# Layer 2: the next image's keys' term in eight steps that begin one chunk earlier, and the choice's subtraction moved from GpSimd to VectorE in seven steps

## The chip, the core and the metric

The kernel runs on one core of a Trainium2 chip. Its engines are TensorE (PE: matmuls; PEld: its weight loads), VectorE (DVE), ScalarE (ACT: activation functions), GpSimd (POOL) and SyncE (SP, which here issues the DMAs). The metric is the device time of one execution in microseconds (us).

## The reference, cut to what matters

A stack of four layers runs on four images of 56 x 56 tokens with 128 channels. The change touches layer 2, and a step that layer 2 and layer 3 share:

```python
def _L2_attn_ref(x, W1, b1, w2, b2):      # x: layer-normalized tokens of an image
    f = jnp.einsum('bih,ha->bia', x, W1[:h])          # the queries' term
    g = jnp.einsum('bjh,ha->bja', x, W1[h:])          # the keys' term
    t = jnp.tanh(f[:, :, None, :] + g[:, None, :, :] + b1)
    scores = jnp.einsum('bija,a->bij', t, w2[:, 0]) + b2[0]
    flag = jnp.tril(jnp.ones((n_seq, n_seq), dtype=x.dtype), -1)[None, :, :]
    e = jnp.exp(scores) * flag
    w = e / (jnp.sum(e, axis=-1, keepdims=True) + 1e-10)
    return jnp.einsum('bij,bjh->bih', w, x)

def _L2_ffn_ref(x, gate_w, gate_b, weight1, weight2):
    probs = jax.nn.softmax(logits, axis=1)            # over an image's tokens, 64 experts
    vals, idx = jax.lax.top_k(probs.transpose(0, 2, 1), K)   # each expert's 8 tokens
    pooled = jnp.einsum('bked,bke->bed', gathered, topv)
    ...
```

Every pair of a query and an earlier key takes 16 tangents, so an image of 3136 tokens costs some 79 million of them.

## The kernel before, in words

**The attention.** An image is 28 tiles of 112 tokens. Queries go in four chunks of seven tiles (784 columns), k = 0 to 3, and for each chunk the key tiles J run from 0 to the chunk's last tile: 7, 14, 21 and 28 of them. Keys lie by eights on the partitions (8 keys x 16 hidden values), so a key tile is 14 groups; four quarters q of a key tile have 4, 4, 3 and 3 of them. A quarter is a *piece*; there are 280 pieces to an image and 1120 in all. For J past the chunk's first tile the causal mask cuts off queries, and the pieces get narrower by 112 columns with each J, from 784 down to 112.

A piece goes through four engines. `adds` (line 1004, DVE) writes up to four sums of the queries' term `fT` and one column of the keys' term `g` into a buffer `th`, of which there are three. `tangents` (L1013, ACT) takes the tanh in place. `scores` (L1024, PE) multiplies by w2 and gathers the rows into a PSUM tile. Once per J, `weights` (L1035 and L1038, ACT) takes the exponential, POOL multiplies the diagonal tile by the mask (L1042), and `weighted` (L1051, PE) sums the values, in quarter 1 of the next J.

**The order.** The program order of these engines is written out by hand in one loop over the pieces. For piece i it issues `tangents(i)`, then at most one extra step, then `adds` of piece i + 2, then `scores(i)`, then (in quarters 0 and 1) `weights` or `weighted` of the J before. The extra step is taken from three lists:

```python
if now and not held:
    now.pop(0)()
elif later_on and q % 2 and not held:
    later_on.pop(0)()
elif behind:
    step = behind.pop(0)
    step()
    held = step.holds
```

`now` holds the end of the chunk before (two copies and four additions to the image, from quarter 2 of J 0 on) and the queries' term of the next chunk of the same image (at J 2). `later_on` is served in odd quarters only. `behind` holds the choice of the image before, filled at J 2 of chunk 0 of images 1 to 3, and in image 3 the experts' matmuls after it.

**`prepare_image`** makes what the next image needs: 14 steps of statistics, a root (`rstd`: ACT loads another table for the square root, and back), 14 steps of normalization into `xa`, seven turns into `xT` (four PE transposes into the PSUM bank "m" and a copy that goes to DVE and ACT by turns, L141 and L143), a memset on POOL and `keys`: eight matmuls of 128 x 392, which read every eighth column of `xT`, into "m", and the addition of b1 on DVE (L972). An fp32 matmul shows as two passes in the trace. The 38 steps come at J 2 of the last chunk, k = 3, with the queries' term of the next image behind them. `xT` has one buffer. The first image is prepared ahead of the loop.

PSUM is full: one bank "m", one bank "h", four for the scores, two for the weighted sums. "h" serves the choice and the experts through `hold`, the fourth of `pools`.

**`choose_steps`** makes an image's choice of tokens in two halves of slots, one slot for each extra step. The first half normalizes, turns and multiplies by the gate. The second, on tiles of 64 experts x 3136 tokens, takes the largest value (slot 1), the exponential, the shares and the eight largest (`eight`, slot 7), replaces those by zero in a copy `M` (`replaced`, slot 8, L1266), and subtracts the copy from the shares, so that `M` keeps the chosen values alone (`left`, slot 9, L1271 on POOL); `M` then goes to DRAM over SP's queue (L1272). Slots 10 and up normalize the tokens again (`norm`, L1219; `c_xa` has three buffers), turn `M` (L1278, copied by ACT, L1284) and pool the tokens (`pool`, L1291); a `norm` waits for the `pool` that frees its buffer. The tiles of the width of an image, `wide`, have two buffers, which the experts' weights (L1330, 1 MB each, over SP) use afterwards. The choice of image 3 is made in layer 3, where a slot that does not hold takes two units of that layer's loop.

Of the kernel before, what the change touches and what calls it, by code (L numbers as in the profile page):

```python
# [17 lines left out]
B, HW, C = 4, 56, 128  # L18
S = HW * HW
P = 128  # L20
# [3 lines left out]
CH = TC * TP  # L24
NCH = S // CH
# [18 lines left out]
JG = P // AH  # L44
# [62 lines left out]
class Hybrid:  # L107
# [764 lines left out]
    def layer2_attention(self):  # L872
# [3 lines left out]
        nc, a, tc = self.nc, self.a, self.tc  # L876
        ET = mybir.EngineType
        with ExitStack() as ctx:
# [5 lines left out]
            wg = self.t(wp, [P, JG, P], "wg")  # L884
# [3 lines left out]
            for j in range(JG):  # L888
                own = slice(j * AH, (j + 1) * AH)
# [12 lines left out]
            ps_h = ctx.enter_context(tc.tile_pool(name="l2_h", bufs=1, space=PSUM))  # L902
# [3 lines left out]
                tc.manual_schedule(engines={ET.PE, ET.Activation, ET.DVE, ET.Pool})  # L906
            )
            m = lambda: self.t(ps_m, [P, 512], "m")
            pools = self.f2_wide, self.f2_sm, m, lambda: self.t(ps_h, [P, 512], "h")
            self.w2 = self.experts2_weights(self.f2_w, m)  # L910
            root = lambda var: self.rstd(sm, var, [TP, NT], 1e-5, "ln")
            im, fT, po, ps, th, es = {}, {}, {}, {}, {}, {}

            chunks = [(t, min(WT, NT - t)) for t in range(0, NT, WT)]
            order = [(b, k) for b in range(B) for k in range(len(chunks))]
# [12 lines left out]
            def halves(lo, hi):  # L928
                return [(i // HALF, max(lo - i, 0), HALF) for i in range(0, hi, HALF) if lo < i + HALF]

            def prepare_image(b):

                r = im[b] = {}
                x = self.X[b]

                def stats(t0):
                    if t0 == 0:
                        r["xa"] = self.t(big, [TP, NT, C], "xa")
                        r["mv"] = self.t(sm, [TP, NT, 2], "ln_mv", bufs=1)
                    for t in range(t0, t0 + 2):  # L940
                        st = self.t(sm, [TP, nc.vector.BN_STATS_DIM], "ln_st", bufs=4)
                        nc.vector.bn_stats(st, x[:, t, :])
                        nc.vector.bn_aggr(r["mv"][:, t, :], st)

                def root():
                    r["r"] = self.rstd(sm, r["mv"][:, :, 1], [TP, NT], 1e-5, "ln")

                def norm(t0):
                    for t in range(t0, t0 + 2):
                        nc.vector.tensor_scalar(  # L950
                            r["xa"][:, t, 0:C], x[:, t, :], r["mv"][:, t, 0:1], r["r"][:, t : t + 1],
                            op0=ALU.subtract, op1=ALU.mult,
                        )

                def turn(c):
                    if c == 0:
                        r["xT"] = self.t(big, [P, S], "xT", bufs=1)
                    self.transposed_chunk(ps_m, "m", r["xa"], c, r["xT"][:, c * CH : (c + 1) * CH])

                def ones():  # L960
                    nc.gpsimd.memset(r["xa"][:, :, C - 1 : C], 1.0)

                def keys():
                    ps = m()
                    for j in range(JG):
                        nc.tensor.matmul(
                            ps[:, : S // JG], wg[:, j, :],
                            r["xT"].rearrange("p (g j) -> p g j", j=JG)[:, :, j],
                            start=(j == 0), stop=(j == JG - 1),
                        )  # L970
                    r["g"] = self.t(big, [P, S // JG], "g")
                    nc.vector.tensor_scalar(r["g"], ps[:, : S // JG], b1, None, op0=ALU.add)  # L972

                bind = lambda f, *args: lambda: f(*args)
                return (
                    [bind(stats, t) for t in range(0, NT, 2)] + [root]
                    + [bind(norm, t) for t in range(0, NT, 2)] + [bind(turn, c) for c in range(NCH)]
                    + [ones, keys]
                )

            def queries(j):

                b, k = order[j]
                t, n = chunks[k]
                fT[j] = self.t(sm, [P, WT * TP], "fT")
                for i, _, w in halves(0, n * TP):
                    ps = m()[:, :w]
                    at = t * TP + i * HALF
                    nc.tensor.matmul(
                        ps, wf.rearrange("p j a -> p (j a)"), im[b]["xT"][:, at : at + w],  # L990
                        start=True, stop=True,
                    )
                    nc.vector.tensor_copy(fT[j][:, i * HALF : i * HALF + w], ps)
# [15 lines left out]
            def tangents(i):  # L1009
                j, J, q = pieces[i]  # L1010
                lo, hi = span(j, J)
                own = th[i][:, 0 : len(groups(q)), lo:hi]
                nc.scalar.activation(own, own, AF.Tanh)  # L1013

            def scores(i):
                j, J, q = pieces[i]
                if q == 0:
                    ps[j, J] = self.t(ps_s, [P, 2, 512], "s")
                off = QW - JG - JG * q
                z = th.pop(i)  # L1020
                for h, lo, hi in halves(*span(j, J)):
                    for blk, n in groups(q):
                        rows = min(QW, TP - QW * blk)
                        nc.tensor.matmul(  # L1024
                            ps[j, J][QW * blk : QW * blk + rows, h, lo:hi], place[:, off : off + rows],
                            z[:, blk, h * HALF + lo : h * HALF + hi],
                            start=(q == 0), stop=(n + 1 == NG or q == TC - 1),
                        )
# [48 lines left out]
            now, later_on, behind, held = [], [], [], False  # L1077
# [4 lines left out]
            def add_ahead(i):  # L1082
                if i < len(pieces):
                    j = pieces[i][0]
                    if i == first[j] and j not in fT:
                        while later_on:
                            later_on.pop(0)()
                        queries(j)
                    adds(i)
# [3 lines left out]
            for i, (j, J, q) in enumerate(pieces):  # L1093
                tangents(i)
                b, k = order[j]
                if J == 2 and q == 0 and j + 1 < len(order):
                    if order[j + 1][1]:
                        now.append(lambda j=j: queries(j + 1))
                    else:
                        later_on += prepare_image(order[j + 1][0])  # L1100
                        later_on.append(lambda j=j: queries(j + 1))
                if k == 0 and J == 2 and q == 0 and b:


                    behind += self.choose_steps(
                        b - 1, self.f2_pooled[:, :, b - 1], self.w2, pools, root
                    )
                    if b == B - 1:
                        behind += self.experts2_steps(
                            range(B - 1), self.f2_pooled, self.w2, pools, 3, lambda: None  # L1110
# [10 lines that stand above are left out]
                add_ahead(i + 2)  # L1121
                scores(i)
                before = pieces[i - TC][:2] if i >= TC else None
                if before and q == 0:
                    weights(*before)
                if before and q == 1:
                    weighted(*before)
                    if before[0] != j:
                        now += attended(before[0])
            j, J, _ = pieces[-1]  # L1130
# [64 lines left out]
    def choose_steps(self, b, pooled, w, pools, root):  # L1195


        nc = self.nc
        wide, sm, m, hold = pools
        x = self.X[b]  # L1200
        r = {}
        bind = lambda f, *args: lambda: f(*args)
# [64 lines left out]
                out=r["M"], in_to_replace=r["top"], in_values=r["pr"], imm_value=0.0  # L1267
            )

        def left():  # L1270
            nc.gpsimd.tensor_sub(r["M"], r["pr"], r["M"])  # L1271
            nc.sync.dma_start(out=w["M"][b], in_=r["M"])  # L1272

        def turn_places(c):
            r["pm", c] = m().rearrange("p (k e) -> p k e", k=TC)
# [20 lines left out]
        def pooled_out():  # L1296
            nc.vector.tensor_copy(pooled, r["pp"][:, :E2])

        over = lambda f: [bind(f, c) for c in range(NCH)]
# [3 lines left out]
            (15, 2, over(logits)), (16, 2, over(biased)),  # L1303
        )
        second = self.in_line(
            (1, 2, [largest, exp, shares, eight]), (8, 1, [replaced]), (9, 1, [left]),
            (10, 2, over(norm)), (13, 2, over(turn_places), True), (14, 2, over(turned_places)),
            (16, 2, over(pool)), (30, 1, [pooled_out]),
        )
        return first + second  # L1310

# [471 lines left out]
```

## Time and profile before

| | us |
|---|---|
| runs shown (3): median, lowest, highest | 8102.83, 8095.14, 8106.98 |
| profiled execution: its time, its span | 8105.82, 8104.0 |
| busy in the span: PE, PEld | 6852.8, 2722.9 |
| busy in the span: DVE, ACT, POOL | 5831.0, 5182.0, 2999.5 |
| layer 2: first to last tangent | 3730 to 6559 |
| tangents L1013, 1120 of 2.09 us | 2294.5 |
| adds L1004, 3920 of 0.56 us | 1935.0 |
| scores L1024, 14336 matmuls | 1490.7 |

The profile is one execution of the program. In the groups of instructions a row gives line, engine, operation, the tile written and the tiles read with their shapes, the count, then the busy time and the mean length of one in ns, then the engine's idle time just before them and what ended most of it. In a timeline a row gives the start, the length, engine, line and operation, the count of those merged, and in brackets the idle time before it and who ended it. A row of windows gives start and end of a stretch, its length, the busy time and number of instructions of PE, PEld, DVE, ACT and POOL, then TensorE's granted clock, the share of DMA engines busy and GB/s.

### The profile page before, as it was taken

The page shows a single profiled execution, that of the slowest core. Times are in us where ns is not written, and L with a number is a line of the kernel's source. Part 1 is how long each engine was busy: PE and PEld are TensorE (multiplying, and loading weights), DVE is VectorE, ACT ScalarE, POOL GpSimd, SP SyncE. Part 2 cuts the span into 40 slices and gives each one's busy share as a digit, 9 for nine tenths or more (in the row PEclk, how much of TensorE's full clock was granted, in tenths as well). Part 3 has the DMA queues.
Part 4 walks back from the last instruction along what each step waited for, and adds up shares of the span by engine and source line. Part 5 has one row for each costly group of instructions (what it writes and reads, how often), then busy time and mean ns, then how long its engine had stood idle before and what let it go on. Part 6 is the DMA issues. An engine that isn't in the chain of part 4 may idle for free.

```text
span 8104.0 us, 106345 instructions
## 1 busy us (share of the span) xinstructions
PE 6852.8 (85%) x41037; PEld 2722.9 (34%) x41037; DVE 5831.0 (72%) x10065; ACT 5182.0 (64%) x5084; POOL 2999.5 (37%) x2081
## 2 busy tenths in 40 slices
PE   8878998999899989996777777777777879999999
PEld 4442333333333333332222222222222334444544
DVE  6777887888788788886787878777787754434444
ACT  4545555556565556555998899889889964333332
POOL 4547887888788788880000000000011000000000
PEclk9989998999899889998999899999989989999999
DMA  2000000000000000000000000000003101210000
GB/s 53 1 13 1 1 1 1 1 1 1 1 1 1 1 1 1 1 1 5 1 1 1 5 1 1 1 5 1 1 26 116 45 6 39 86 63 5 5 6 6
DMA packets 85494, 102.39 MB, mean 13 GB/s; under 512 B 21158, under 2 KB 50742, under 8 KB 84279
## 3 DMA queue, kind: packets, MB, share of 16 engines
q1 hardware_dynamic: 84985, 95.58, 4.0%
q8 instruction: 322, 5.28, 0.3%
q14 instruction: 187, 1.53, 0.1%
HBM read 85.28 MB, written 10.29 MB: 12 GB/s over the span
## 4 chain that ended last, share of the span: by engine, by line
PE 38%; ACT 17%; POOL 15%; issue 14%; DVE 10%; DMA 0%; SPq 0%; ACTq 0%; DVEq 0%; POOLq 0%
ACT th L1013 12%; POOL hs L690 10%; PE q L1555 7%; PE o L1566 6%; PE s L1024 6%; DVE th L1004 5%; POOL dBu L673 4%; PE a L654 3%; PE o L1051 3%; PE pe L1720 2%; PE m L792 2%; PE y L696 1%; PE u L663 1%; PE m L728 1%; DVE hs L685 1%
## 5 line engine op out<-in xcount | busy, mean ns | idle before, releaser
L1013 ACT ACTIVATE th<-th 128x3136 f32<-128x3136 f32 (+12 forms) x1120 | 2294.5, 2094 | 220.1 <-DVE th L1004 166.1
L1004 DVE TENSOR_SCALAR th<-fT,g 128x784 f32<-128x784 f32 (+6 forms) x3920 | 1935.0, 561 | 475.1 <-PE s L1024 442.1
L1024 PE MATMUL s<-th,place 128*32 128x392 f32 (+7 forms) x14336 | 1490.7, 492 | 712.1 <-ACT th L1013 708.9
L685 DVE TENSOR_TENSOR_SCAN hs<-a,dBu 128x896 f32<-128x896 f32 x896 | 1795.8, 2014 | 282.2 <-ACT a L668 272.4
L690 POOL TENSOR_TENSOR hs<-hs,bc 128x896 f32<-128x896 f32 x896 | 1842.2, 2083 | 68.8 <-DVE hs L685 40.3
L668 ACT ACTIVATE a<-a 128x896 f32<-128x896 f32 x896 | 811.4, 906 | 805.4 <-PE u L663 607.4
L663 PE MATMUL u<-du,pick 32*128 32x448 f32 x3584 | 988.2, 626 | 99.2 <-ACT dBu L672 51.8
L654 PE MATMUL a<-delta,A_pick 32*128 32x448 f32 x3584 | 1007.5, 612 | 6.8 <-DVE hs L685 6.1
L1024 PEld LDWEIGHTS s<-th,place 128*32 128x32 f32 (+1 forms) x14336 | 423.8, 111 | 1647.3 <-ACT th L1013 1126.4
L1560 ACT ACTIVATE e<-q,shift 128x448 f32<-128x448 f32 (+1 forms) x700 | 441.5, 634 | 739.8 <-PE q L1555 739.4
L678 DVE TENSOR_TENSOR dBu<-u,bc 128x896 f32<-128x896 f32 x616 | 663.5, 1077 | 168.3 <-PE u L663 167.4
L673 POOL TENSOR_TENSOR dBu<-dBu,bc 128x896 f32<-128x896 f32 x280 | 583.7, 2084 | 434.0 <-ACT dBu L672 434.0
L1566 PE MATMUL o<-e,xk 128*128 128x448 f32 (+1 forms) x1400 | 655.7, 550 | 29.3 <-ACT oT L1541 29.3
L1042 POOL TENSOR_TENSOR e<-e,later 112x112 f32<-112x112 f32 x112 | 79.2, 707 | 1602.3 <-ACT e L1035 968.6
L1555 PE MATMUL q<-xT 128*128 128x448 f32 (+1 forms) x1400 | 658.4, 553 | 7.8 <-ACT e L1560 7.8
L1725 DVE SCALAR_TENSOR_TENSOR X<-pe,r_gate,X 112x128 f32<-112x128 f32 x896 | 313.9, 351 | 462.1 <-PE pe L1720 426.1
L654 PEld LDWEIGHTS a<-delta,A_pick 32*128 32x128 f32 x3584 | 316.4, 193 | 545.4 <-issue 253.8
L696 PE MATMUL y<-hs,sum 128*32 128x448 f32 x3584 | 453.1, 577 | 3.0 <-POOL hs L690 3.0
L1051 PE MATMUL o<-e,xa 112*128 112x392 f32 (+5 forms) x1024 | 425.7, 538 | 1.1 <-POOL e L1042 1.1
L663 PEld LDWEIGHTS u<-du,pick 32*128 32x128 f32 x3584 | 285.8, 193 | 327.4 <-DVE dBu L678 195.0
L1566 PEld LDWEIGHTS o<-e,xk 128*128 128x128 f32 (+1 forms) x1400 | 264.1, 192 | 315.8 <-issue 277.2
L1654 POOL MEMSET lc_xa<- 112x4 f32 x28 | 3.1, 110 | 933.7 <-DVE lc_xa L1648 666.4
(253 smaller groups left out, 7688.0 us busy)
## 6 DMA issues: line engine op xcount, KB each, us to landing
wide<-in_L_ffn_weight SPq DMA_DIRECT2D x64, 1024.0 KB
X<-in_x SPq DMA_DIRECT2D x8, 784.0 KB
out<-X SPq DMA_DIRECT2D x28, 224.0 KB
M<-wide SPq DMA_DIRECT2D x4, 784.0 KB
wide<-M SPq DMA_DIRECT2D x4, 784.0 KB
e_edge<-dtab SPq DMA_DIRECT2D x42, 49.0 KB
cw<-in_L_conv_conv_w SPq DMA_DIRECT2D x1, 1024.0 KB
c_h<-in_L_ffn_weight SPq DMA_DIRECT2D x16, 64.0 KB
```

The source lines that it names most:

```text
L654: nc.tensor.matmul(halves(A[p])[:, k], w["A"][own, order[j][2], f, q, :], pre[j]["delta"][own, f], start=True, stop=True,)
L663: nc.tensor.matmul(halves(U[p + 1])[:, k], w["pick"][own, q, :], pre[j]["du"][own, f], start=True, stop=True,)
L668: nc.scalar.activation(A[p], A[p], AF.Exp)
L673: nc.gpsimd.tensor_mul(v, v, pre[j]["bc"][:, 0:1].to_broadcast([P, 2, CH]))
L685: nc.vector.tensor_tensor_scan(flat, A.pop(p), V.pop(p), 0.0, op0=ALU.mult, op1=ALU.add)
L690: nc.gpsimd.tensor_mul(HS[p], HS[p], bc[:, 1:2].to_broadcast([P, 2, CH]))
L1004: nc.vector.tensor_scalar(th[i][:, blk, lo:hi], fT[j][:, lo:hi], im[order[j][0]]["g"][:, at : at + 1], None, op0=ALU.add,)
L1013: nc.scalar.activation(own, own, AF.Tanh)
L1024: nc.tensor.matmul(ps[j, J][QW * blk : QW * blk + rows, h, lo:hi], place[:, off : off + rows], z[:, blk, h * HALF + lo : h * HALF + hi], s ...
L1051: nc.tensor.matmul(po[j][:, h, lo:hi], im[b]["xa"][:, J, :], e[:, h * HALF + lo : h * HALF + hi], start=(J == 0), stop=(J == t + ((h + 1) ...
L1555: nc.tensor.matmul(ps[:n, :CH], xT[b][:, k : k + n], xT[b][:, c * CH : (c + 1) * CH], start=True, stop=True,)
L1566: nc.tensor.matmul(po[b, c], xk[b][:n, t, :], es.pop((b, c, t))[:n], start=(t == 0), stop=(t == N - 1))
```

## The change

`prepare_image` is put on `later_on` from J 6 of the last chunk but one (k = 2) on, where the choice is done. Its last step becomes nine: eight steps of one matmul each, which accumulate in bank "h" in place of "m", and one for the addition of b1. The queries' term of the next image is still put on the list at J 2 of the last chunk.

In the choice, `left` is split into seven steps of 448 tokens on DVE; the store follows the seventh. `replaced` moves from slot 8 to 10, the seven steps of `left` take slots 11, 13 and so on to 23, and all later stages move by two slots, from a last slot of 30 to one of 32.

```diff
-            pools = self.f2_wide, self.f2_sm, m, lambda: self.t(ps_h, [P, 512], "h")
+            hold = lambda: self.t(ps_h, [P, 512], "h")
+            pools = self.f2_wide, self.f2_sm, m, hold
...
-                def keys():
-                    ps = m()
-                    for j in range(JG):
-                        nc.tensor.matmul(
-                            ps[:, : S // JG], wg[:, j, :],
-                            r["xT"].rearrange("p (g j) -> p g j", j=JG)[:, :, j],
-                            start=(j == 0), stop=(j == JG - 1),
-                        )
+                def keys(j):
+                    if j == 0:
+                        r["ps"] = hold()
+                    nc.tensor.matmul(
+                        r["ps"][:, : S // JG], wg[:, j, :],
+                        r["xT"].rearrange("p (g j) -> p g j", j=JG)[:, :, j],
+                        start=(j == 0), stop=(j == JG - 1),
+                    )
+
+                def keyed():
+                    ps = r["ps"]
                     r["g"] = self.t(big, [P, S // JG], "g")
                     nc.vector.tensor_scalar(r["g"], ps[:, : S // JG], b1, None, op0=ALU.add)
...
-                    + [ones, keys]
+                    + [ones] + [bind(keys, j) for j in range(JG)] + [keyed]
...
                     else:
-                        later_on += prepare_image(order[j + 1][0])
                         later_on.append(lambda j=j: queries(j + 1))
+                if J == 6 and q == 0 and k == len(chunks) - 2 and b + 1 < B:
+                    assert not behind
+                    later_on += prepare_image(b + 1)
...
-        def left():
-            nc.gpsimd.tensor_sub(r["M"], r["pr"], r["M"])
-            nc.sync.dma_start(out=w["M"][b], in_=r["M"])
+        def left(c):
+            own = slice(c * CH, (c + 1) * CH)
+            nc.vector.tensor_sub(r["M"][:, own], r["pr"][:, own], r["M"][:, own])
+            if c == NCH - 1:
+                nc.sync.dma_start(out=w["M"][b], in_=r["M"])
...
-            (1, 2, [largest, exp, shares, eight]), (8, 1, [replaced]), (9, 1, [left]),
-            (10, 2, over(norm)), (13, 2, over(turn_places), True), (14, 2, over(turned_places)),
-            (16, 2, over(pool)), (30, 1, [pooled_out]),
+            (1, 2, [largest, exp, shares, eight]), (10, 1, [replaced]), (11, 2, over(left)),
+            (12, 2, over(norm)), (15, 2, over(turn_places), True), (16, 2, over(turned_places)),
+            (18, 2, over(pool)), (32, 1, [pooled_out]),
```

## The prediction

> **What bounds the kernel now.** The page comes first: which engine is busiest overall does not decide, because the change lies in layer 2 alone, slices 19 to 33 of 40, where the page's slices give ACT eights and nines and PE and DVE sevens and eights. The groups of instructions say what fills ACT there: the tangents.
>
> ```profile
> L1013 ACT ACTIVATE th<-th 128x3136 f32<-128x3136 f32 (+12 forms) x1120 | 2294.5, 2094 | 220.1 <-DVE th L1004 166.1
> ```
>
> There are 1120 pieces, four to a key tile J. I took the start of the first tangent of every J from the timeline: a full-width J (784 query columns) without extra work takes 10.40 us, all of it ACT. Stretches that are longer are what can be won. Windows over three neighbouring J at the passage from image 2 to image 3 (the last chunk, J 20, 21, 22) give busy time by engine:
>
> ```profile
> 5762.20:5772.60 10.40, 7.13 (x56) 2.65 (x52) 8.14 (x15) 9.41 (x6) 0.25 (x1) 1.00 0.01 2
> 5772.60:5794.80 22.20, 20.12 (x92) 5.98 (x92) 6.79 (x13) 11.35 (x7) 0.00 (x0) 1.00 0.00 0
> 5794.80:5803.80 9.00, 7.53 (x51) 2.46 (x48) 7.58 (x16) 8.35 (x4) 0.00 (x0) 1.00 0.01 3
> ```
>
> J 21 takes 22.2 instead of 10.4, with PE full and ACT half idle. The timeline names the cause:
>
> ```profile
> 5780.60 11.51 PE L966 MATMUL m<-xT,wg 128*128 128x392 f32 x16
> 5792.15 0.63 DVE L972 TENSOR_SCALAR g<-m,b 128x392 f32<-128x392 f32 x1 [12.05 <-PE m L966]
> 5793.62 0.91 ACT L1035 ACTIVATE e<-s,b 112x784 f32<-112x784 f32 x1 [10.58 <-PE s L1024]
> ```
>
> The keys' term is 16 matmul passes in one step; the scores queue behind them, and DVE's sum waits for them at the head of its own queue. All three passages (4347, 5063, 5781 us) show J 21 at 22.2.
>
> The choice is read in the same way: the sixth J of chunk 1 in image 1 (first row) against the same J in image 0, which has no choice to make (second row).
>
> ```profile
> 4547.40:4569.60 22.20, 8.50 (x72) 2.56 (x66) 20.95 (x18) 10.68 (x5) 7.06 (x1) 0.86 0.12 25
> 3847.70:3858.10 10.40, 7.32 (x64) 2.36 (x60) 7.80 (x14) 10.40 (x6) 0.00 (x0) 1.00 0.01 2
> ```
>
> Here DVE is full. The timeline again:
>
> ```profile
> 4555.81 3.40 DVE L1266 MATCH_REPLACE8 wide<-c_top,wide 64x3136 f32<-64x3136 f32 x1
> 4559.14 10.38 DVE L1004 TENSOR_SCALAR th<-fT,g 128x784 f32<-128x784 f32 x7
> 4559.35 7.06 POOL L1271 TENSOR_TENSOR wide<-wide 64x3136 f32<-64x3136 f32 x1 [81.24 <-DVE wide L1266]
> 4567.49 4.97 ACT L1013 ACTIVATE th<-th 128x2352 f32<-128x2352 f32 x2 [9.41 <-DVE th L1004]
> ```
>
> Seven adds take 10.38 us where they take 3.85 elsewhere; one of them has the length of POOL's subtraction (the longest add of the kernel is 7.17 us). ACT is idle 9.41. It recurs at 5276 and 5993.
>
> **What the Trainium skill says.** SBUF — State Buffer, "Reading the diagram": DVE and GpSimd share a port pair under an exclusive lock, and the loser waits for the whole instruction. The trace agrees: an add of 0.6 us lasts 7.17 beside the 7.06 us subtraction. Perfetto Trace Analysis, "Optimizing Scalar/DVE Operations": breaking up an instruction that causes bubbles elsewhere may let work finish sooner. The 10.58 us bubble is of that kind, though on PE. VectorE: DVE Perf Modes, the section on the TRN2 errata, prices an fp32 sum of two tensors at (N+151)/0.96 ns: an estimate of 624 ns for 448 columns. The trace has no such row on DVE; its rows of 28 columns (0.186 us) and 896 (1.068) interpolate to 0.61. Neighbours overlap (the 784-wide add reads 0.63 and comes every 0.56), so I take 0.56 on the queue.
>
> **The change part by part.** Sums are against the profiled execution: 8105.82 us, a span of 8104.0 and 1.8 around it, 3.0 above the median of 8102.83.
>
> 1. *Keys in eight steps.* Two passes each, 11.51/8 = 1.44 us, on every second piece. A plain full-width J has PE at 7.3 of 10.4, so two steps make 10.2. A step in quarter 1 lies in PE's wait for the tangent (1.99 us there in the timeline); in quarter 3 it follows the weighted sum (1.58) and the scores (1.17), and PE ends its scores 6.9 us after quarter 1's tangent, just before ACT needs them at 7.0. I take +0.5 per image (0 if all is hidden, 4 if the granted clock drops to the 0.86 seen above). Against it J 21 loses its 11.8; the queries' matmuls and copies move from there to about J 9 of the last chunk and keep some 0.6. Net -10.7 per image, -32 for three. The first image's keys run before the loop, unchanged. The sum on DVE (0.63) comes two pieces after the last matmul and waits no more. The bank "h" is otherwise used by the choice, long finished; nothing queues for it.
>
> 2. *Preparation begins in chunk 2.* From J 6 there are 30 odd quarters to J 20: 14 statistics, the root, 14 normalizations, the first turn. Statistics and normalizations at full width are free today: such J still take 10.4 with DVE at 9.1. The root's 2.9 us (two table loads of 1.28) only moves. New is what falls into the narrowing J 15 to 20: two steps of 0.60 us per J. Windows over J 18 and 19, then J 20, of chunk 2, image 0:
>
> ```profile
> 4097.10:4107.10 10.00, 7.39 (x77) 2.44 (x74) 7.94 (x28) 9.06 (x11) 0.97 (x2) 1.00 0.01 2
> 4107.10:4111.90 4.80, 2.48 (x39) 0.94 (x33) 4.49 (x15) 2.57 (x5) 0.42 (x1) 1.00 0.00 0
> ```
>
> DVE has some 1 us to spare per J up to J 19 and 0.3 in J 20. I take 0.2 + 0.5 + 1.0, and 0.5 each for turns 0 and 1: +2.7 per image (0.5 if the gaps take all, 7 if none), +8 in all. POOL's mask multiply there waits longer for the port (3.39 us at worst beside the choice now); a piece and more lies before its reader.
>
> 3. *The turns change quarter.* A turn whose copy is ACT's costs 1.5 us in quarter 3 (idle 1.0, copy 0.53) but about 0.5 in quarter 1. Windows over J 16 to 19 of the last chunk:
>
> ```profile
> 4288.90:4336.30 47.40, 34.24 (x280) 12.18 (x277) 34.43 (x65) 43.42 (x24) 0.24 (x1) 1.00 0.00 1
> 5009.00:5052.20 43.20, 33.27 (x271) 11.54 (x265) 33.36 (x63) 42.92 (x25) 0.00 (x0) 1.00 0.00 1
> ```
>
> Images 1 and 3 (first row) have ACT's four in quarter 3; turns 2, 4, 6 now fall in quarter 1: 6.0 becomes 1.6, -4.4 twice. Image 2 goes the other way: 1.6 becomes 3.7, +2. Sum -7.
>
> 4. *The subtraction.* J 6 loses the 7.06 block and part of what the match-replace, which now comes two free pieces later, stacked on the max: from 22.2 to about 14 (10.4, some 2 each for max and match-replace), -8.2. Added are 7 x 0.56 = 3.9 us on DVE, in J 7 to 10, where DVE with normalizations stands near its limit (9.9 of 10.8 in J 7, 8.3 of 9.6 in J 8), so all of it counts; and everything after slides by half a J into narrower pieces, where normalizations wait for the pooling matmuls up to 3.5 us: +1.4. Net -3 per image (between -8, additions hidden, and +2, waits doubled), -9. The store of the choice leaves after the seventh step, some 35 us later on SP, and ahead of the first expert weights in image 3 (6000.5, then about 6035); their first matmul is at 6057.8, which leaves cover for the megabyte; without it a few us once. In layer 3 the same block stands at 6757, with DVE at 33 of 64 us in that chunk: -2, and the later steps slide by four units, across no chunk's start.
>
> Sum: -32 + 8 - 7 - 9 - 2 = -42, from 8105.8 to 8064 profiled, **8061** for the median.
>
> **The rivals.**
> - *More comes back.* Narrow gaps take the preparation (-6), the subtractions hide in gaps (-13): -61, about 8042. For it: DVE waits for scores between its adds. Against: in J 20 DVE is the limit today.
> - *PE is the next wait.* Eight steps at a low granted clock cost 1.4 each, as one block did: the 32 is gone but for a few us, and -6 to -13 remains, 8090 to 8097. For it: the quarter-3 margin of 0.1 us. Against: two turns per J already fit PE in image 2.
> - *Slower: the ring of three "th" buffers has no slack.* Place: every odd quarter. Each inserted step then delays the tangents by its length: keys 11.5 per image (nothing won there), normalizations and turns in narrow J 7, subtractions 3.9 and the slide 5 against 7.1: with the turns, +7 per image, 8124. It decides once DVE plus PE latency around the ring passes three pieces. Against: full-width J with statistics stay at 10.4.
> - That the edit does not do what it says is hardly open: the step positions follow from the lists.
>
> **How the numbers follow.** A difference under 0.2% (16 us) can't be told from none. The forecast has 0.70, "more" 0.17, "PE next" 0.08 (within 0.2% or just outside), "ring" 0.05: faster 0.88, same 0.07, slower 0.05. The unknown costs give -42 +/- 20; the range runs 8036 to 8088, leaving out much of "PE next" and all of "ring".
>
> **What would show it.** Right: J 21 of the last chunk near 10.5; the keys' matmuls in pairs over J 5 to 8 with those J at 10.4 to 11; no add over 1 us in chunk 1; J 6 of chunk 1 near 14, with J 7 to 11 together some 5 us longer; J 18 to 20 of chunk 2 up 2 us. Wrong: J 5 to 8 of the last chunk at 12 or more, J 15 to 20 up by 7, or J 7 to 11 taking back the whole gain of J 6.

## The result, and the profile after

| | before | after |
|---|---|---|
| median (lowest to highest), us | 8098.99 (8087.33 to 8106.98) | 8042.18 (8037.23 to 8051.22) |
| profiled execution: span | 8104.0 | 8037.1 |
| start to first tangent (layers 0 and 1) | 3730.1 | 3714.2 |
| first to last tangent (layer 2) | 2829.4 | 2790.9 |
| last tangent to end (layer 3) | 1544.6 | 1532.0 |

The changed kernel takes 0.9932 of the time before, 95% interval 0.992 to 0.9944: 45 to 65 us less. The two profiles differ by 67, but 15.9 of that lies in layers 0 and 1, which the change does not touch. What belongs to the change in them is 38.4 in layer 2 and 12.6 in layer 3, together 51.

The passage from image 2 to image 3, in windows over J 20, 21 and 22 of the last chunk (start and end, length, then the busy time and number of instructions of PE, PEld, DVE, ACT and POOL, TensorE's clock, DMA share, GB/s):

```profile
5731.50:5741.90 10.40, 7.31 (x66) 2.36 (x60) 7.80 (x14) 10.40 (x6) 0.00 (x0) 1.00 0.00 1
5741.90:5752.20 10.30, 7.21 (x54) 2.45 (x48) 7.57 (x14) 10.30 (x6) 0.00 (x0) 0.87 0.01 2
5752.20:5762.90 10.70, 8.41 (x60) 2.96 (x60) 6.82 (x14) 9.32 (x6) 0.46 (x1) 0.82 0.00 0
```

J 21 is back at 10.3, all of it ACT. The keys now lie in J 5 to 8, two steps to a J, one hidden and one half in the open. The timeline around the start of J 6, where line 967 is a step of the keys:

```profile
5575.51 1.65 PE L967 MATMUL h<-xT,wg 128*128 128x392 f32 x2
5577.08 2.83 PE L1028 MATMUL s<-th,place 128*32 128x392 f32 x28
5578.66 0.92 ACT L1039 ACTIVATE e<-s,b 112x784 f32<-112x784 f32 x1 [0.72 <-PE s L1028]
5579.85 1.65 PE L967 MATMUL h<-xT,wg 128*128 128x392 f32 x2
5582.33 1.52 PE L1028 MATMUL s<-th,place 128*32 128x392 f32 x16 [0.83 <-ACT th L1017]
```

The first step stands in quarter 3: the scores come 1.57 us later and ACT's exponential (L1039) waits 0.72 for them. The second stands in quarter 1: PE still waits 0.83 for ACT after it. Windows over J 7 and J 10 show what follows, 11.2 and 14.6 in place of 10.4 (in image 1 they take 11.2 and 13.9); in J 10 the granted clock is 0.88:

```profile
5586.30:5597.50 11.20, 10.37 (x67) 3.13 (x64) 7.80 (x14) 10.47 (x6) 0.00 (x0) 1.00 0.01 2
...
5621.10:5635.70 14.60, 10.99 (x73) 3.49 (x70) 8.75 (x16) 10.64 (x6) 0.00 (x0) 0.88 0.00 0
```

J 10 holds the queries' term of the next image. In image 1 its timeline reads:

```profile
4922.07 0.93 PE L993 MATMUL m<-xT,wf 128*128 128x392 f32 x2
4923.03 0.57 DVE L997 COPY fT<-m 128x392 f32<-128x392 f32 x1 [1.47 <-PE m L993]
4923.65 0.93 PE L993 MATMUL m<-xT,wf 128*128 128x392 f32 x2 [0.66 <-DVE fT L997]
4924.51 2.83 PE L1028 MATMUL s<-th,place 128*32 128x392 f32 x28
...
4926.09 0.91 ACT L1039 ACTIVATE e<-s,b 112x784 f32<-112x784 f32 x1 [1.59 <-PE s L1028]
```

The scores behind the step start 2.4 us after it does; inside it PE waits 0.66 for DVE's copy. The step is in quarter 3 again.

The choice in image 1, windows over J 6 and J 7 of chunk 1, and the timeline from the match-replace on:

```profile
4528.60:4541.30 12.70, 8.60 (x72) 2.61 (x66) 11.36 (x17) 10.53 (x5) 0.00 (x0) 1.00 0.00 1
4541.30:4554.50 13.20, 8.15 (x48) 2.56 (x48) 12.58 (x22) 10.62 (x7) 0.00 (x0) 0.76 0.01 1
```

```profile
4540.87 3.40 DVE L1272 MATCH_REPLACE8 wide<-c_top,wide 64x3136 f32<-64x3136 f32 x1
...
4544.20 2.22 DVE L1008 TENSOR_SCALAR th<-fT,g 128x784 f32<-128x784 f32 x4
4546.35 0.60 DVE L1278 TENSOR_TENSOR wide<-wide 64x448 f32<-64x448 f32 x1
4546.51 6.97 ACT L1017 ACTIVATE th<-th 128x3136 f32<-128x3136 f32 x3 [1.58 <-DVE th L1008]
```

J 6 takes 12.7 instead of 22.2 and J 7 13.2 instead of 10.8; ACT's wait of 9.4 is one of 1.6, and no add in chunk 1 lasts over 0.73 us.

### The profile page after: what moved, and what is told of

It is laid out like the page before. It is cut to its first block, busy times and chain, and to the rows that moved or that the text cites. A ratio compares the mean times of both kernels' runs of the same rounds, so it can differ in the third digit from the quotient of the medians.

```text
span 8037.1 us, 106369 instructions
## 1 busy us (share of the span) xinstructions
PE 6835.5 (85%) x41037; PEld 2717.5 (34%) x41037; DVE 5818.5 (72%) x10093; ACT 5183.5 (64%) x5084; POOL 2975.3 (37%) x2077
## 3 DMA queue, kind: packets, MB, share of 16 engines
q14 instruction: 187, 1.53, 0.1%
## 4 chain that ended last, share of the span: by engine, by line
PE 38%; ACT 17%; POOL 15%; issue 14%; DVE 10%; DMA 0%; SPq 0%; ACTq 0%; DVEq 0%; POOLq 0%
ACT th L1017 13%; POOL hs L690 10%; PE q L1563 7%; PE o L1574 7%; PE s L1028 6%; DVE th L1008 5%; POOL dBu L673 4%; PE o L1055 3%; PE a L654 2%; PE pe L1728 2%; PE m L792 2%; PE y L696 1%; PE u L663 1%; PE m L728 1%; POOL du L839 1%
```

## The experiments

Stages are read from one profile of each kernel, in the three stretches of the table above. Medians and ratios are against the kernel before on the same chip.

| kernel | median | ratio, interval | layers 0, 1 | layer 2 | layer 3 |
|---|---|---|---|---|---|
| keys_only | 8084.45 | 0.9983 (0.9975 to 0.9990) | 3720.0 | 2809.5 | 1544.6 |
| left_only | 8067.21 | 0.9967 (0.9954 to 0.9979) | 3718.3 | 2805.9 | 1532.0 |
| after_again | 8041.51 | 0.9930 (0.9918 to 0.9942) | 3713.7 | 2794.0 | 1532.0 |
| l3_old | 8051.81 | 0.9940 (0.9927 to 0.9954) | 3723.8 | 2790.6 | 1545.4 |
| l3_late | 8090.41 | 0.9991 (0.9982 to 1.0000) | 3721.6 | 2828.0 | 1537.1 |
| left_dve1 | 8077.86 | 0.9976 (0.9966 to 0.9985) | 3722.8 | 2807.8 | 1541.0 |
| left_whole | 8059.01 | 0.9948 (0.9933 to 0.9963) | 3716.5 | 2801.2 | 1532.1 |
| left_pool7 | 8045.22 | 0.9937 (0.9921 to 0.9954) | 3719.3 | 2790.5 | 1534.9 |
| keys_late | 8051.65 | 0.9945 (0.9930 to 0.9960) | 3719.4 | 2799.9 | 1532.2 |
| keys_q1 | 8019.76 | 0.9903 (0.9886 to 0.9919) | 3720.9 | 2760.0 | 1531.4 |
| queries_two | 8048.19 | 0.9939 (0.9924 to 0.9954) | 3732.1 | 2796.7 | 1530.3 |
| both | 8024.63 | 0.9906 (0.9891 to 0.9921) | 3725.1 | 2769.4 | 1533.7 |

**How sharp a stage is.** Layers 0 and 1 are the same code in all fourteen profiles and take 3713.7 to 3732.1: a difference of 15.9 there is scatter. In layer 2 a J with the same steps repeats within 0.1 us, but for single J that are longer, by up to 2.2 us, and that are not the same ones in all runs. One such J is 14 of image 0's chunk 2 in the kernel before, at 12.3; just ahead of it PE's weighted sum takes 2.98 instead of 1.58, where TensorE's granted clock is 0.52:

```profile
4058.00:4060.90 2.90, 2.90 (x9) 1.18 (x4) 2.24 (x4) 2.87 (x2) 0.00 (x0) 0.52 0.00 0
4058.37 2.98 PE L1051 MATMUL o<-e,xa 112*128 112x392 f32 x4
```

Sums over layer 2 of the same code are thus good to some 5 us; a single J is good to 0.1 where the clock is full in both profiles.

### Each part alone, and the whole again

`keys_only` is the changed kernel with `left` and the slots of before; `left_only` is the kernel before with the new `left` and slots; `after_again` is unaltered.

keys_only, expected: 

> The changed preparation alone; the choice stays as before (one subtraction on POOL). Theory read from the two traces (the preparation is worth 6.5 us an image): J 21 of the last chunk at 10.3 instead of 22.2, J 6 to 9 of the last chunk 0.8 longer each, J 10 some 3.5 longer (the queries' step), J 6 of chunk 1 still 22.2 with an add of 7.2 us; layer 2 shorter by 13 to 20 us, ratio about 0.998. Rival, the prediction's own sizes (keys -32, narrow pieces +8, turns -7): layer 2 shorter by 31 us, ratio about 0.996.

left_only, expected: 

> The changed choice alone; preparation and keys as before. Theory read from the two traces (the choice is worth 7 us an image in layer 2): J 6 of chunk 1 at 12.7 instead of 22.2, J 7 +2.3, J 8 +1.4, no add over 1 us in chunk 1, layer 2 shorter by 19 to 22 us, layer 3 shorter by 5 to 13 us, ratio 0.996. Rival, the prediction's own size: layer 2 shorter by 9 us, layer 3 by 2, ratio 0.9985. J 21 of the last chunk stays at 22.2.

after_again, expected: 

> The changed kernel, unaltered, on the same chip as the others. If the 15.9 us by which layers 0 and 1 differ between the two profiles is scatter, the stretch ahead of the first tangent differs here by another amount, while the J of layer 2 repeat within 2 us per image and the sum of layer 2 stays near -38; layer 3 shows whether -12.6 repeats. Ratio 0.993 to 0.995. If instead the two edits add up, ratio of this one is the product of the other two within 0.001.

The preparation gives 6.6 us an image: layer 2 is 19.9 shorter, with J 21 -11.8, J 6 to 9 about +0.8 each, J 10 +3.4 to 4.5, and the turns' changes; layer 3 is the same to 0.1. The first theory holds; the prediction's 31 lies outside the interval of the ratio, 8 to 20 us. The choice gives 6.9, 3.4 and 6.8 us in chunk 1 of the three images (7.2, 7.0 and 7.0 in the changed kernel): J 6 -9.6, J 7 +2.3, J 8 +1.4, the rest about -1 in images 1 and 3. Layer 2 is 23.5 shorter and layer 3 12.5. The prediction's 9 and 2 were too little. The repeat gives -35.4 and -12.6. The product of the two ratios, 0.9950, is 0.002 above the 0.9930 of the whole, more than the 0.001 expected; the stages say the opposite, the two parts giving 8 us more in layer 2 than the whole. Whether the parts add up exactly stays open.

### Where layer 3's 12.6 us come from

`l3_old` gives image 3's choice its old form back within the changed kernel; `l3_late` puts two empty slots after it in the kernel before:

```diff
-            for steps, num in ((chosen, 4), (passed, 2)):
+            for steps, num in ((chosen + self.in_line((1, 1, [lambda: None])), 4), (passed, 2)):
```

l3_old, expected: 

> The changed kernel, in which the choice of image 3, made in layer 3, keeps the old form: one subtraction on POOL and the old slots. If the gain of layer 3 comes from the choice there, layer 3 is as long as before (about 1544 us from the last tangent to the end, 12 more than the changed kernel), ratio 0.995. If it is scatter, layer 3 stays near 1532 and the ratio at 0.993.

l3_late, expected: 

> The kernel before, with two empty slots after the choice of image 3 in layer 3, so that the experts' steps there begin four units later, as they do in the changed kernel; the subtraction stays on POOL. Theory A (layer 3 gains by where the experts' steps fall against the chunk's end): chunks 5 to 9 shorten as in the changed kernel, 59.0, 57.2, 58.1, 58.2, 58.6 to 56.9, 57.7, 57.1, 55.4, 55.0, while chunk 3 stays at 64.0; layer 3 shorter by about 8 us. Theory B (it gains by the subtraction itself): layer 3 as before, within 1 us.

`l3_old` is back at 1545.4: the gain is the choice's. `l3_late`, which only lets the experts begin four units later, gains 7.5 of it: chunk 3 stays at 64.0, and chunks 5, 8 and 9 take 56.9, 55.4 and 55.0 as in the changed kernel instead of 59.0, 58.2 and 58.6. This is theory A. The timeline at the start of chunk 8 says why; first the kernel before, then `l3_late`. L1370 is the experts' matmul, L1566 the first weighted sum of the new chunk, which must wait until DVE and ACT have copied the old one out.

```profile
7057.65 0.92 PE L1555 MATMUL q<-xT 128*128 128x448 f32 x2
...
7060.91 1.02 PE L1566 MATMUL o<-e,xk 128*128 128x448 f32 x2 [2.34 <-ACT oT L1541]
7061.85 1.93 PE L1370 MATMUL h<-wide,z 128*32 128x512 f32 x8
```

```profile
7043.92 1.07 PE L1370 MATMUL h<-wide,z 128*32 128x512 f32 x8
7044.92 1.02 PE L1555 MATMUL q<-xT 128*128 128x448 f32 x2
...
7047.08 1.02 PE L1566 MATMUL o<-e,xk 128*128 128x448 f32 x2 [1.14 <-ACT oT L1541]
```

Before, the matmuls come after PE's wait; four units later in the list they are ahead of it and fill it. The first five units of the chunk take 14.8 instead of 17.6. The block on POOL is the other part: with the subtraction on DVE at the old slot (`left_dve1`, next), layer 3 loses 3.6, in chunks 2 and 3. Of the 12.6, some 1.5 are left to neither.

### What of the choice gives the gain

`left_dve1` changes one word in the kernel before, `nc.gpsimd` to `nc.vector`. `left_whole` keeps the changed slots and puts the subtraction into the first of the seven as one instruction. `left_pool7` keeps the seven steps and gives them to POOL.

```diff
-            nc.vector.tensor_sub(r["M"][:, own], r["pr"][:, own], r["M"][:, own])
+            if c == 0:
+                nc.vector.tensor_sub(r["M"], r["pr"], r["M"])
```

left_dve1, expected: 

> The kernel before with the subtraction in one instruction on DVE at its old slot right after the match-replace. Theory (the engine is worth the difference of 7.1 and an estimated 3.4 us, the split and the two free slots the rest): J 6 of chunk 1 at about 18.5 instead of 22.2, layer 2 shorter by 11 us, about half of what the changed choice gives. Rival (the engine alone does it): J 6 near 15, layer 2 shorter by 20.

left_whole, expected: 

> The changed kernel with the subtraction in one DVE instruction (64x3136, some 3.4 us) at the slot of the first of the seven; all other slots as changed, so it follows the match-replace by one slot and that one follows the max by three. Theory (the free slots and the engine give the gain, since the seven steps cost about as much DVE time as the one): J 6 of chunk 1 at 12.6, J 7 at 15.5 to 16.5 instead of 13.2, J 8 to 10 together 2 to 3 us shorter; layer 2 within 3 us of the changed kernel. Rival (the split hides the 3.9 us in DVE's gaps): layer 2 longer by 6 to 11 us.

left_pool7, expected: 

> The changed kernel, but the seven steps of the subtraction on POOL instead of DVE, in the same slots. Theory (POOL's tensor operation holds DVE up for its own length, some 1.0 us for 448 columns against 0.56 of DVE's queue): adds of 1.2 to 1.6 us beside each step, J 7 to J 10 of chunk 1 together 2 to 4 us longer than in the changed kernel, layer 2 6 to 12 us longer. Rival (only the one block of 7 us hurt; in pieces POOL's work lies beside DVE's): J 7 to 10 2 to 4 us shorter than in the changed kernel.

The engine alone brings J 6 to 19.1: -3.2 there, -3.3 to -3.7 over chunk 1, about half of the 7. In its timeline DVE's two long instructions still stand one adds apart, and ACT waits after each:

```profile
4543.97 3.40 DVE L1266 MATCH_REPLACE8 wide<-c_top,wide 64x3136 f32<-64x3136 f32 x1
...
4548.91 3.41 DVE L1271 TENSOR_TENSOR wide<-wide 64x3136 f32<-64x3136 f32 x1
4549.10 2.16 ACT L1013 ACTIVATE th<-th 128x2352 f32<-128x2352 f32 x1 [2.86 <-DVE th L1004]
...
4554.58 2.82 ACT L1013 ACTIVATE th<-th 128x3136 f32<-128x3136 f32 x1 [3.32 <-DVE th L1004]
```

With the two free slots ahead of the match-replace and the subtraction still whole, J 6 is at 12.6 to 12.7 as in the changed kernel: that J is won by the engine and the slots. The split is seen after it: J 7, at 14.9, is 1.7 longer than with seven steps, though less than expected, and over J 6 to 8 it is 1.3 to 1.7. Over the whole of chunk 1 the difference is 2.3 in image 2, where both kernels have the full clock in J 9 and 10, 4.1 in image 1, where `left_whole` has a lowered clock in J 10 (0.72), and 0.2 in image 3, where the changed kernel has one in J 9 (0.85). So where the clocks are alike the split is worth some 2 us an image, about a third of the choice's 7. Layer 2 is 10.3 longer, 6.5 of it in chunk 1; by that sum the rival (6 to 11) is met and the theory (3) is not, and the lowered clock is too uneven to say how much of it is the split's. The median's ratio, 0.9948, lies 0.0016 to 0.0018 above that of the changed kernel.

On POOL a step lasts 1.18 us, and adds beside them up to 1.53; but POOL does not keep to the slots. Its only wait here is the one for the match-replace, and the first three steps follow one another at once:

```profile
4548.31 6.49 DVE L1008 TENSOR_SCALAR th<-fT,g 128x784 f32<-128x784 f32 x7
4548.46 4.30 POOL L1278 TENSOR_TENSOR wide<-wide 64x448 f32<-64x448 f32 x3 [84.59 <-DVE wide L1272]
4553.28 6.92 ACT L1017 ACTIVATE th<-th 128x3136 f32<-128x3136 f32 x3 [4.23 <-DVE th L1008]
```

J 7 is 2.7 longer than in the changed kernel. J 8 to 11, where DVE has those steps no more, are together as much shorter in images 1 and 3, but 1.0 in image 2, where the changed kernel has the full clock there. Layer 2 is the same, 2790.5, and so is the time (0.9937): DVE's wait beside POOL is there as expected, the 6 to 12 us are not, and in the sum these runs do not tell the two engines apart once the subtraction is in seven steps.

### What of the keys gives the gain, and what is left in it

`keys_late` keeps the eight steps and starts the preparation at J 2 of the last chunk, as before. `keys_q1` puts an empty step after each of the eight; `queries_two` makes the queries' term in two steps; `both` does the two.

```diff
-                    + [ones] + [bind(keys, j) for j in range(JG)] + [keyed]
+                    + [ones] + [f for j in range(JG) for f in (bind(keys, j), lambda: None)][:-1] + [keyed]
...
-                        later_on.append(lambda j=j: queries(j + 1))
+                        later_on += [lambda j=j, i=i: queries(j + 1, i) for i in range(2)]
```

keys_late, expected: 

> The changed kernel, but the preparation begins at J 2 of the last chunk as before; the eight steps of the keys then fall into J 21 to 24, pieces of 784 down to 448 columns, and the sum and the queries behind them. Theory (what counts is to have PE's block in pieces; where they lie decides how much of each 1.5 us is seen, and in narrower pieces PE has less to spare): J 21 near 12 instead of 22.2, J 22 to 25 together 4 to 7 us longer than before; layer 2 3 to 12 us longer than the changed kernel. Rival (the split alone does it all): layer 2 within 2 us of the changed kernel.

keys_q1, expected: 

> The changed kernel with an empty step after each of the keys' steps, so that all eight fall into quarter 1, over J 5 to 12 of the last chunk. Theory (a step in quarter 1 lies in PE's wait for the tangents; the 0.8 us per J are those of quarter 3, behind the weighted sum): no J of the last chunk longer for the keys, layer 2 shorter than the changed kernel by 8 to 10 us. Rival (PE is simply too full, each step costs 0.4 wherever it stands): 0.4 us on each of eight J, no gain.

queries_two, expected: 

> The changed kernel with the queries' term of a chunk in two steps, one half each, wherever it is made. Theory (the 3.5 us at J 10 of the last chunk are PE's wait, in one step, for DVE's copy of the first half out of the single bank m): J 10 of the last chunk at 10.4 to 11 instead of 14, -3 per image; at J 2 of the other chunks up to -0.9; layer 2 shorter by 9 to 15 us. Rival (it is the two matmuls and copies themselves): the 3.5 spread over J 10 and 11, no gain.

both, expected: 

> The two together: keys in quarter 1 alone, queries' term in two steps. If both theories hold, layer 2 is 17 to 25 us shorter than that of the changed kernel, some 8020 us, ratio to the kernel before 0.9905.

`keys_late`: J 21 at 11.2 (-11.0), and J 22 to 25 longer by 1.3, 1.7, 1.7 and 1.6. The split alone saves 11.0 there and gives back 6.3 in the narrow J, -4.7 in all; in the changed kernel J 6 to 10 and J 21 make -5.1. For the keys and the queries, then, the early start gains next to nothing. Layer 2 is nonetheless 9.0 longer than in the changed kernel, as expected in size but not for the stated reason: the turns stay in J 16 to 19 and in their old quarters, and their change of quarter is what the early start brings (about 8 us over three images, less 2 in the narrow J, see below; the rest of the 9.0 is within the scatter).

`keys_q1`: windows over J 6 to 9 and 10 to 12 of image 2's last chunk:

```profile
5563.80:5605.50 41.70, 35.66 (x254) 10.62 (x248) 31.19 (x56) 41.70 (x22) 0.00 (x0) 1.00 0.00 1
5605.50:5636.80 31.30, 26.76 (x192) 8.01 (x189) 23.63 (x43) 31.30 (x16) 0.00 (x0) 1.00 0.00 1
```

These are seven J at 10.4, with ACT busy all the time: in quarter 1 the keys cost nothing. The queries' term, pushed on to J 13, falls into quarter 1 as well and costs 0.9 instead of 3.5. Together 5.8 us an image, 17 in all, where 8 to 10 were expected; the profile's 31 also hold some J with a lowered clock fewer. At 0.9903 (0.9886 to 0.9919) its median is the lowest here.

`queries_two` takes 2.8 off J 10 as expected, but the additional step shifts the choice's slots in chunks 0 and 1 (J by J from -2.4 to +2.8), and nothing is left in the sum. `both` lands where expected, layer 2 21.5 us shorter than in the changed kernel, but `keys_q1` alone reaches 31.0: the split of the queries adds nothing to it.

## Why the prediction was right, and where it was not

The direction, the two mechanisms and the time within the range were right. The sum of 42 against 51 in the stages owes its fit to errors that cancel.

1. *Keys, predicted -32, measured about -15.* The 11.8 of J 21 came back to the tenth. Two terms were too small. The eight steps: 0.5 an image was taken, 3.2 measured (0.8 on each of four J), inside the stated bounds of 0 to 4. The margin of quarter 3 was mis-sized. Its 6.9 us come out as 1.52 + 1.58 + 1.17 + 1.44 + 1.17, counted from the end of quarter 1's tangents: scores, weighted sum, scores, step, scores. The 1.17 matches a row that the edge of a window at 5765 cuts; whole, as it stands first below, it reads 1.52, and the scores of a quarter with three groups (12 matmuls) take as long as those with four (16). Before:

```profile
5764.33 1.52 PE L1024 MATMUL s<-th,place 128*32 128x392 f32 x16 [1.45 <-ACT th L1013]
5765.78 1.58 PE L1051 MATMUL o<-e,xa 112*128 112x392 f32 x4
5767.29 1.52 PE L1024 MATMUL s<-th,place 128*32 128x392 f32 x12
```

   With 1.45 from one row of scores to the next in place of 1.17, and 1.57 in place of 1.44, the sum is 7.6, past the 7.0 at which ACT needs the scores; the exponential waited 0.72. The queries: 0.6 was taken; in quarter 3 they cost 3.5, with a clock of 0.88 in J 10 (in two steps 2.8 less, by `queries_two`, though its layer 2 kept none of it). The chance of the rival "PE is the next wait" was too low: in quarter 3 it is what happened, at about half its price of 1.4 a step, and at the full clock (1.00 in J 7).
2. *Narrow J, predicted +8, measured about +2.* J 19 and 20 are 0.2 and 0.5 longer, J 15 to 18, where the clock is full, not at all: DVE's waits for the scores take the normalizations, as "more comes back" had it. J 14 is 2.0 shorter in the profile, but also in `left_only` and `l3_late`, where its steps are unchanged; it doesn't count.
3. *Turns, predicted -7, measured about -8.* The images are those that are prepared, the J those of the last chunk ahead of them. Images 1 and 3: 1.5 off each of four J, 0.4 on each of three or four. Image 2: 1.5 off in the sum of J 17 to 19, and 1.5 on each of J 2 and 3, so +1.4 where +2 was expected. (The profile of before has J 2 at 11.7 as well, but with a clock of 0.71; in `left_only`, `l3_late` and `keys_late`, which have the same steps there, it takes 10.4.)
   By single J these three make -21; layer 2 of `keys_only` is 19.9 shorter.
4. *The choice in layer 2, predicted -9, measured about -21.* J 6 lost 9.6 rather than 8.2, since the match-replace, to which 2 us were given there, now begins only 0.4 us before J 6 ends (4540.87): ACT's 1.58 behind it is part of J 7's +2.3. "All of it counts" was the wrong term for the additions: with that 1.58 in it, J 7 to 12 are 2.7 longer, so 3.9 us of DVE work and the slide leave about 1 an image, not 5.3.
5. *Layer 3, predicted -2, measured -12.6.* The sentence that failed is that the later steps slide "by four units, across no chunk's start". It asked only where the steps end. What counts is on which side of PE's wait at each chunk's start a step stands: -7.5 by `l3_late`. The block itself was worth 3.6, not 2.

Together the parts make some -55 by single J, against -51 in the stages. The landing at 8042, where "more comes back" stood, is thus not that rival's: two of its terms were right, the keys gave half, and the rest came from layer 3. That the profile of before lay 15.9 above that of after in layers 0 and 1 is scatter, and no part of the change: the repeat and `queries_two`, both with the changed preparation, stand at 3713.7 and 3732.1 there.

## What to carry to other kernels

When a long step is dealt out over a loop, ask for each piece not only whether its engine has room in the period but where in the period it lands: the same 1.6 us of PE were free in quarter 1 and cost 0.8 behind the weighted sum, and a turn copied by ACT 0.4 or 1.5. When steps of a list move, look at every regular wait that they pass, also in a stage that the change does not mean; a shift by four units was worth more than half of layer 3's gain. A row at the edge of a window may be cut: take a length from a row that stands inside it. And read a gain stage by stage against stages that did not change, before adding it up.

## What the runs showed of the hardware

- A step's place in the list does not hold an engine back: POOL, given seven steps dealt out over fourteen slots, ran three of them back to back (4.30 us) and DVE's adds beside them were slow (seven adds in 6.49 us where 3.85 is usual, single ones up to 1.53).
- TensorE's granted clock drops for a few us (0.52 over 2.9 us at 4058 in the kernel before) at places that are not all the same from run to run, and a J there can take about 2 us more (12.3 or 12.6 instead of 10.4); with the same code, layer 2 took 2790.9 and 2794.0.
- The scores of three groups, 12 matmuls of 128x392 with 32 columns of weights, take PE as long as those of four, 16 matmuls: 1.52 us each.
